# Turning every list's rows with TensorE's transposes, in a graph layer with a mixture of experts

## The chip, the core and the metric

The kernel runs on one core of a Trainium2 chip, in one launch. The metric is device time in microseconds (us), the median of several executions. Five engines work side by side, each through its own instructions in order: TensorE (PE, with its weight loads shown as PEld), VectorE (DVE), ScalarE (ACT), GpSimd (POOL) and SyncE (SP). DMA transfers are issued from SP's and POOL's streams.

## What is computed

3,327 tokens of 256 features pass a graph attention layer and then a mixture of 16 experts, of which each token uses two. Cut to what matters (`_layernorm` without scale and shift; everything in float32):

```python
# graph layer, on h = _layernorm(x) @ W, 4 heads of 64
attn = softmax(where(adj > 0, e, -9e15))       # e depends on the row and the head alone
x = x + layernorm(attn @ h) * gamma + beta
# experts, on x_n = _layernorm(x)
probs = softmax(x_n @ gate_w + gate_b)
top_probs, top_idx = top_k(probs, 2)           # two experts a token
hidden = silu(x_n @ w1[e]) * (x_n @ w2[e])     # 256 -> 512, for each expert e
x = x + sum over the token's two experts of  weight * (hidden @ w3[e])
```

## The kernel before

**The graph layer.** Tokens lie in 26 tiles of 128, in 7 groups. The adjacency matrix is streamed in and multiplied with `h` split in two parts (lines 598 and 599); after each group its rows are finished, normalized, gated and stored to a DRAM tensor `normed`, and their numbers are put into lists by expert.

**The lists.** The experts' work is cut into 19 lists of token numbers, 0 to 18, with room for `ROOM[i]` tokens (line 89). Lists 0 to 2 hold the tokens of three experts from the first five groups, lists 3 to 5 those of the same experts from the last two, and lists 6 to 18 (480, 472, 416 and so on down to 336 tokens from list 8 on) the other 13 experts, the fullest first. `take_list` (line 1143) writes the work of one list:

- *Gather* (line 970): one indirect DMA on POOL for each tile of 128 rows, from `normed` into one of three buffers (`XE[i % 3]`). A weighing on DVE (lines 976 and 978) takes the tokens' weights from the gathered rows.
- *Turning*: the products need the rows with features on partitions. Lists 0 to 7 use TensorE's transposes (line 1174) into a bank of PSUM, two of 128 x 128 for each tile of rows, and ACT copies each half (k = 0, 1) to the tile `xt` (line 1183). Lists 8 to 18 go through `by_halves` (line 1116): ACT and DVE split the 32-bit words into 16-bit halves (lines 1137 and 1138), SP issues a DMA transpose for each tile (line 1128), and ACT and DVE join the halves in `xt` (lines 1140 and 1141). `TURNED = 2 * EARLY + 2 = 8` is the first list that does so.
- *Up products*: lists 0 to 5 plainly (line 985). Lists 6 to 18 use seven products in the place of eight for each pair of column blocks (`by_sevenths`, line 996), two pairs a list, after a scheme that needs four sums of the weights and four of `xt` on DVE (line 1018). In a pair, p1, p5, p6, p2, p7, p3, p4 form a chain through copies on ACT (line 1052) and sums on DVE (line 1056): p6 needs p1's copy, p7 a sum of p6 and p5, p4 a copy of p7. p1, p6 and p7 write a bank of the pool `pt`, of two banks, which the transposes use as well.
- *Gate*: ACT's silu (line 1078) and DVE's product (line 1081) make `hid`.
- *Down products* (line 1099; a last tile of 64 rows or fewer packs its matmuls side by side, line 1095): for each tile of 128 rows into one of two `ph` banks. ACT scales full tiles by the tokens' weights to `y` (line 1222), DVE the small ones (lines 1224 and 1226); there are six `y` buffers.
- *Scatter* (line 1102): one indirect DMA on POOL for each tile adds `y` to the output's rows. A list's scatters follow the landing of the list before, since two lists may hold the same token.

A list's weights (1.5 MB) are loaded from SP's stream into one of four buffers.

**What sets the order.** Every step is added to a plan (class `Plan`, line 116) with an engine, a cost, a rank, what it follows and which buffers it takes. The planner places at each turn the step that can start first by these costs; rank decides between steps that can start together (lower goes first). It tries 80 orders, keeps the one that ends first in replays, and the instructions are then written in that order, each engine following its own. A cost thus changes no instruction, only its place. The rank of list i's down products is `(4, i + 1, 9, t)` from list 6 on (line 1212), that of its up products `(4, i, pair, number)`: the down products of list i fill gaps of the chain of list i + 1 and come behind it.

Of the kernel before, what the change touches and what calls it, by code (L numbers as in the profile page):

```python
# [77 lines left out]
CT = CAP // P  # L78
EARLY = 3
EARLY_GROUP = 4  # L80
TURNED = 2 * EARLY + 2

SEVEN = 2 * EARLY

NL = NE + EARLY
LIST = 4096
NR = NE - EARLY

# [130 lines left out]
def gnn_moe(ctx: ExitStack, tc: tile.TileContext, x, adj_t, W, a, gamma, beta, gate_w, gate_b, w1, w2, w3, out):  # L219
    nc = tc.nc  # L220
# [54 lines left out]
    column = const.tile([P, P], F32, name="column")  # L275
    piece = const.tile([P, NL, CT], F32, name="piece")
    code = const.tile([P, NT], F32, name="code")
    listed = const.tile([P, NL, CT], F32, name="listed")
    nc.vector.memset(listed, 0.0)
# [3 lines left out]

    count = const.tile([P, NL], F32, name="count")
    expert = const.tile([P, NL], F32, name="expert")
    behind = const.tile([P, NL], F32, name="behind")
    end = const.tile([P, NL], F32, name="end")
    room = const.tile([P, NL], F32, name="room")
# [6 lines left out]
    def constants():  # L295
# [10 lines left out]

        ramp(base, [[0, 2], [LIST // P, NE]], 0, 0)
        ramp(base[:, 1, :EARLY], [[LIST // P, EARLY]], NE * LIST // P, 0)

        ramp(column, [[1, P]], 0, 0)  # L310
        ramp(piece, [[LIST // P, NL], [1, CT]], 0, 0)
        ramp(expert[:, :2 * EARLY], [[0, 2], [1, EARLY]], 0, 0)
        for k in range(2):
            ramp(behind[:, k * EARLY:(k + 1) * EARLY], [[LIST, EARLY]], k * NE * LIST, 0)
        for i, n in enumerate(ROOM):
# [34 lines left out]
    PE, DVE, ACT, POOL, SP = "PE", "DVE", "ACT", "POOL", "SP"  # L350
# [61 lines left out]
    plan = Plan(SLOTS, take)  # L412
# [470 lines left out]
    def all_lists(counted, lists):  # L883
# [46 lines left out]
        def rest():  # L930
# [5 lines left out]
            nc.vector.tensor_reduce(count[:, 2 * EARLY:], by, AX.X, ALU.add)  # L936
            nc.vector.tensor_scalar(behind[:, 2 * EARLY:], expert[:, 2 * EARLY:], float(LIST), None, op0=ALU.mult)
            nc.vector.tensor_scalar(end, behind, float(LIST), None, op0=ALU.add)
            nc.vector.tensor_add(behind, behind, room)
# [56 lines left out]
    def by_sevenths(i, n, xts, loaded, fixed, xtk, wk, hk, weights):  # L996

        half = n // 2
        xsk, wsk, ask = ("xsum", i), ("hp", "list", i), ("agg", "list", i)
# [20 lines left out]
        def sums(cost, rank, after, uses, terms):  # L1020
            done, got = {}, []
            for k, (name, dst, one, other, op, needs) in enumerate(terms):
                done[name] = plan.add(DVE, cost, rank, after + [done[x] for x in needs],
                                      lambda dst=dst, one=one, other=other, op=op: combine(dst, one, other, op), uses)
            return done

        S = sums(0.62, (2, i, 7), loaded, [wk, wsk, ask], [
            ("1", lambda: ws(0), lambda: a(1, 0), lambda: a(1, 1), ALU.add, ""),
            ("2", lambda: ws(1), lambda: ws(0), lambda: a(0, 0), ALU.subtract, "1"),
            ("3", lambda: a(1, 0), lambda: a(0, 0), lambda: a(1, 0), ALU.subtract, "1"),  # L1030
            ("4", lambda: ws(2), lambda: a(0, 1), lambda: ws(1), ALU.subtract, "2")])
        X_ = sums(0.1 + 0.55e-3 * n, (2, i, 6), xts, [xtk, xsk, ask], [
            ("1", lambda: xs(0), lambda: b(0, 1), lambda: b(0, 0), ALU.subtract, ""),
            ("2", lambda: xs(1), lambda: b(1, 1), lambda: xs(0), ALU.subtract, "1"),
            ("3", lambda: b(0, 1), lambda: b(1, 1), lambda: b(0, 1), ALU.subtract, "1"),
# [2 lines left out]
        hids = []  # L1038
# [77 lines left out]
    def by_halves(i, got, tiles, xek, xtk, opened):  # L1116

        hk, tk = ("halves", i), ("turned", i)
        nt, m = len(tiles), len(tiles) * P

        def words(h):
            return XE[i % 3][:, :nt, :D].bitcast(U16).rearrange("p t (d h) -> p t d h", h=2)[:, :, :, h]

        def halves_of(h):
            return T[hk][:, :nt, h, :]

        def turn(t):
            nc.sync.dma_start_transpose(out=T[tk][:, :, t * P:(t + 1) * P], in_=T[hk][:, t].rearrange("p h d -> p (h d)"))

        def joined(h):  # L1130
            return T[xtk].rearrange("p (a b) k q -> p a (b k q)", a=KC).bitcast(U16).rearrange(
                "p a (n h) -> p a n h", h=2)[:, :, :m, h]

        def turned(h):
            return T[tk][:, h * KC:(h + 1) * KC, :m]

        s = [plan.add(ACT, 0.1 + 0.23 * nt, (1, i), got + opened[:1], lambda: nc.scalar.copy(halves_of(0), words(0)), [xek, hk]),
             plan.add(DVE, 0.1 + 0.15 * nt, (2, i, 8), got + opened[:1], lambda: nc.vector.tensor_copy(halves_of(1), words(1)), [xek, hk])]  # L1138
        w = [plan.add(SP, 1.3, (1, i), s, lambda t=t: turn(t), [hk, tk], landing=2.7, size=2 * P * D * 4) for t, _ in tiles]
        return [plan.add(ACT, 0.1 + 1.25e-3 * m, (1, i), w, lambda: nc.scalar.copy(joined(0), turned(0)), [tk, xtk], slack=2.0),  # L1140
                plan.add(DVE, 0.1 + 1.3e-3 * m, (2, i, 8), w, lambda: nc.vector.tensor_copy(joined(1), turned(1)), [tk, xtk], slack=2.0)]

    def take_list(i, indexed, stored, weights, opened, order):

        n = ROOM[i]
        tiles = row_tiles(n)
        xek, xtk, hk, wk = ("xe", i), ("xt", "list", i), ("hid", i), ("w", weights)
        limit = NP if i >= EARLY else (GROUPS[EARLY_GROUP][-1] + 1) * P
        rank = (4, i)
# [8 lines left out]
        def w_of(k):  # L1158
            return WE[weights][k]

        got = GOT[i] = [plan.add(POOL, 1.33, (1, i), [indexed] + stored, lambda t=t: gather(XE[i % 3], index_of(i), t, limit), [xek],
                        landing=2.6) for t, _ in tiles]
# [9 lines left out]
        def turned(k):  # L1172
            for t, _ in tiles:
                nc.tensor.transpose(psum(("pt", "list", i, k))[:, t * P:(t + 1) * P], XE[i % 3][:, t, k * P:(k + 1) * P], ident)

        m = len(tiles) * P
        xts = []
        if i >= TURNED:
            xts = by_halves(i, got, tiles, xek, xtk, opened)
        for k in range(KC if i < TURNED else 0):  # L1180
            key = ("pt", "list", i, k)
            w = plan.add(PE, 0.13 * len(tiles), rank + (0,), got, lambda k=k: turned(k), [key, xek])
            xts.append(plan.add(ACT, 0.1 + 0.9e-3 * m, (1, i), [w], lambda k=k, key=key: nc.scalar.copy(
                xt()[:, k, :m], psum(key)[:, :m]), [key, xtk]))
        hids = []
        if i >= SEVEN:
            if i == SEVEN:
                CHAIN.append(plan.add(PE, 0.9, (4, i, -1), UPS, fix_banks, [("pa", "fixed", r) for r in range(4)]))
            hids = by_sevenths(i, n, xts, opened, CHAIN[0], xtk, wk, hk, weights)
        for j in range(JC if i < SEVEN else 0):  # L1190
# [12 lines left out]
            s = plan.add(ACT, 0.1 + 0.95e-3 * n, (1, i), [ups[0]], gate, [keys[0], ("gate", i, j)])  # L1203
            hids.append(plan.add(DVE, 0.1 + 1.1e-3 * n, (2, i), [s, ups[1]], both, [keys[1], ("gate", i, j), hk]))
        ends = []
        for t, mm in tiles:
            key, yk = ("ph", "list", i, t), ("y", i, t)
            parts = (0, 1) if i >= SEVEN and PARTS[mm] == 1 else (None,)
            w = None
            for part in parts:  # L1210
                w = plan.add(PE, (8 * 0.217 / PARTS[mm] + 0.1 * (PARTS[mm] > 1)) / len(parts),
                             (4, i + 1, 9, t) if i >= SEVEN else rank + (9 + t,), hids + [w],
                             lambda t=t, mm=mm, key=key, part=part: down_products(psum(key), w_of(2), hid(), t, mm, part),
                             [key, hk] + ([wk] if weights else []))


            helped = (i < EARLY or i >= SEVEN) and PARTS[mm] == 1

            def scale(t=t, mm=mm, key=key, yk=yk, helped=helped):
                weight = T["weight", i][:mm, t:t + 1]  # L1220
                if helped:
                    nc.scalar.mul(T[yk][:mm], psum(key)[:mm, :D], weight)  # L1222
                else:
                    nc.vector.tensor_scalar(T[yk][:mm], psum(key)[:mm, :D], weight, None, op0=ALU.mult)
                for c in range(P // PARTS[mm], P, P // PARTS[mm]):
                    nc.vector.scalar_tensor_tensor(T[yk][:mm], psum(key)[c:c + mm, :D], weight, T[yk][:mm],
                                                   op0=ALU.mult, op1=ALU.add)

            w = plan.add(ACT if helped else DVE, 0.48 * PARTS[mm], (2, i), [w, wd], scale, [key, yk, ("weight", i)])
            ends.append(plan.add(POOL, 1.87, (1, i), [w] + order, lambda t=t, mm=mm, yk=yk: add_rows(  # L1230
                T[yk], index_of(i, out_index), t, mm, others, i < EARLY), [yk], landing=2.5))
# [13 lines left out]
    for t in range(GT):  # L1245
        LOADED[0, t] = plan.add(SP, 0.45, (0, t), [], lambda t=t: load_x(0, t, t + 1), landing=2.0, size=P * D * 4)
        if t == 0:
            got = plan.add(SP, 0.45, (0, t), [], lambda: nc.sync.dma_start(
                a_rows, bass.AP(tensor=a.tensor, offset=a.offset, ap=[[DH, 2], [1, DH]])), landing=2.0, size=512)
# [7 lines left out]
    for made, c0, c1, c in ((landed, H, H + D, 1.0), (summed, 0, H, 0.5)):  # L1257
        means, subtract = center(w_sb, ("ph", "w", c0), c0, c1)
        w = plan.add(PE, c, (0,), [made], means, [("ph", "w", c0)])
# [11 lines left out]
    w = plan.add(PE, 0.8, (2,), [rest], means, [("ph", "gw")])  # L1271
# [7 lines left out]
    for g in range(NG):  # L1279
# [3 lines left out]
        s, c, l, d = finish(g, terms, add_beta(g, read[g]), tables)  # L1283
# [3 lines left out]
        if g == EARLY_GROUP:  # L1287
            i, c = early_lists(c, l)
            tables = [c]
            ready.update({k: (i, list(stored)) for k in range(EARLY)})  # L1290
        if g == NG - 1:
            i, ranked, o = all_lists(c, l)
# [22 lines left out]
    opened = plan.add(PE, 0.0, (9,), every, switch_pools)  # L1315
# [23 lines left out]
    with tc.If(many["value"] > 0):  # L1339
        with tc.For_i(0, NL) as i:  # L1340
            e = nc.values_load(table[0:1, 0, bass.ds(i, 1)], min_val=0, max_val=NE - 1)
            full = nc.values_load(table[0:1, 1, bass.ds(i, 1)], min_val=0, max_val=1)
            w = weight_tiles()
            load_weights(w, e)
            with tc.For_i(0, full * (NT // AGAIN)) as c:
# [11 lines left out]
                n = AGAIN * P  # L1357
# [6 lines left out]
                for j in range(JC):  # L1364
# [3 lines left out]
                    s = POOLS["gates"].tile([P, CAP], F32, name="s")  # L1368
# [42 lines left out]
```

## Time and profile before

| | |
|---|---|
| median of three executions | 529.54 us (526.9 to 530.24) |
| the profiled execution | 529.58 us, of which 527.4 from its first to its last instruction (the span) |
| mean granted TensorE clock | 0.982 of full speed |
| the lists' gathers, line 970 | 61, 1,078 ns mean on POOL, 4.7 us median to landing |
| the scatters, line 1102 | 61, 1,661 ns mean on POOL, 4.3 us median to landing |
| DMA transposes, line 1128 | 41, 3.6 us median to landing |
| TensorE's transposes, line 1174 | 40, 277 ns mean |
| copies from PSUM to `xt`, line 1183, 128 x 512 | 4, 588 ns mean |
| splitting, 128 x 1024 halves | ACT 1,044 ns, DVE 714 ns mean |
| joining, 128 x 1024 halves | ACT 1,335 ns, DVE 773 ns mean |

The profile is one execution on the chip. Its page gives the busy time of each engine, the span in 40 equal slices (a digit is the busy share of a slice in tenths; PEclk is the granted clock), and groups of equal instructions. The trace gives windows (the same for any stretch) and the timeline: start, duration, engine, line, operation, destination and sources, and in brackets how long the engine stood before the row and what ended that. Matmuls follow each other closer than their durations say, because they are pipelined; a float32 product is shown as two matmuls, a transpose as one. Releasers are inferred, and a few matmul records are missing.

### The profile page before, as it was taken

Reading aid. Unit: us, or ns where it says so; the run is one execution under the profiler, and the core shown is the slowest. Engines: PE = TensorE matmul, PEld = TensorE weight load, DVE = VectorE, ACT = ScalarE, POOL = GpSimd, SP = SyncE. Lnnn points to the kernel's source line nnn. Section 1 sums busy time; section 2 is a strip of 40 time slices with the busy share of each in tenths; the row PEclk is TensorE's granted clock in tenths of the full one; section 3 lists DMA queues with packets and bytes.
Section 4 is the critical chain, followed back from the end, with each engine's and each line's share of the span. In section 5 each row is a group of like instructions: output and inputs, shape, how many; then the busy total and the mean of one; then the engine's idle time right before and its main releaser. Section 6 shows DMA issues by size and latency. Waiting matters only on the chain. (4 is left out here: it accounts for less than half of the span.)

```text
span 527.4 us, 9541 instructions
## 1 busy us (share of the span) xinstructions
PE 497.3 (94%) x3239; PEld 449.5 (85%) x3240; DVE 349.0 (66%) x1035; ACT 235.2 (45%) x637; POOL 222.1 (42%) x240
## 2 busy tenths in 40 slices
PE   9999999999999999999999799898799989999991
PEld 6789999999999999777778589797688879989990
DVE  5978563977869799679844496646548656877320
ACT  2452154536371760573222466545435454454440
POOL 4220022211031412756786578365375544444333
PEclk9999999999999999999999899999989998999996
DMA  8933879797869895563399659594595877642222
GB/s 273 356 131 101 291 268 293 255 332 240 276 209 367 263 370 157 196 183 99 64 293 322 95 134 118 159 211 78 167 215 83 210 238 170 131 122 30 24 30 34
DMA packets 85703, 100.06 MB, mean 190 GB/s; under 512 B 27150, under 2 KB 59154, under 8 KB 85652
## 3 DMA queue, kind: packets, MB, share of 16 engines
q1 hardware_dynamic: 74612, 85.42, 51.9%
q0 software_dynamic: 10768, 13.75, 16.2%
q8 instruction: 26, 0.43, 0.3%
q10 hardware_dynamic: 272, 0.26, 0.1%
q14 instruction: 25, 0.20, 0.1%
HBM read 81.55 MB, written 13.75 MB: 181 GB/s over the span
## 5 line engine op out<-in xcount | busy, mean ns | idle before, releaser
L598 PE MATMUL pa<-hi,mk 128*128 128x258 f32 x676 | 167.6, 289 | 0.0
L599 PE MATMUL pa<-lo,mk 128*128 128x256 f32 x676 | 163.2, 282 | 0.0
L1102 POOL DMA_INDIRECT out<-y,out_index x61 | 101.3, 1661 | 106.2 <-ACT y L1222 68.8
L598 PEld LDWEIGHTS pa<-hi,mk 128*128 128x128 f32 x676 | 127.9, 189 | 1.1 <-issue 1.0
L599 PEld LDWEIGHTS pa<-lo,mk 128*128 128x128 f32 x676 | 127.7, 189 | 0.1
L1099 PE MATMUL ph<-w3e,hid 128*128 128x256 f32 (+5 forms) x400 | 97.2, 386 | 7.1 <-ACT y L1222 7.0
L1099 PEld LDWEIGHTS ph<-w3e,hid 128*128 128x128 f32 (+5 forms) x400 | 74.3, 190 | 18.6 <-ACT y L1222 9.0
L970 POOL DMA_INDIRECT x<-normed,index x61 | 65.8, 1078 | 27.7 <-issue 18.0
L575 DVE TENSOR_SCALAR mk<-sg 128x2048 fp32r<-128x2048 f32 (+2 forms) x49 | 54.2, 1106 | 28.9 <-PE pa L599 28.2
L1046 PE MATMUL pt<-xt,w12e 128*128 128x256 f32 (+8 forms) x208 | 47.4, 353 | 2.2 <-DVE pa L1056 2.2
L1078 ACT ACTIVATE s<-pa 128x256 f32<-128x256 f32 (+8 forms) x78 | 26.8, 345 | 43.6 <-PE pa L1046 41.4
L1046 PEld LDWEIGHTS pt<-xt,w12e 128*128 128x128 f32 x208 | 37.4, 194 | 7.0 <-DVE pa L1056 2.9
L664 POOL TENSOR_TENSOR hp<-csum,c 128x512 f32<-128x512 f32 (+1 forms) x14 | 15.1, 1096 | 65.0 <-DVE c L660 65.0
L1081 DVE TENSOR_TENSOR hid<-s,pa 128x256 f32<-128x256 f32 (+8 forms) x78 | 28.8, 371 | 14.7 <-ACT s L1078 13.6
L1222 ACT ACTIVATE y<-ph,weight 128x256 f32<-128x256 f32 (+4 forms) x50 | 23.1, 470 | 33.0 <-PE ph L1099 31.7
L1052 ACT COPY pa<-pt 128x512 f32<-128x512 f32 (+8 forms) x52 | 25.1, 498 | 17.8 <-PE pt L1046 15.3
L1056 DVE TENSOR_TENSOR c<-pt,qs 128x512 f32<-128x512 f32 (+8 forms) x26 | 15.5, 596 | 25.5 <-ACT pa L1052 25.5
L492 PE MATMUL ph<-w_sb,xnt 128*128 128x260 f32 x104 | 27.9, 405 | 0.6 <-DVE lo L498 0.6
L985 PE MATMUL pa<-xt,w12e 128*128 128x352 f32 (+3 forms) x128 | 26.8, 360 | 0.0
L1046 PE MATMUL pa<-xsum,w12e 128*128 128x256 f32 (+8 forms) x104 | 22.9, 343 | 1.6 <-ACT pa L1052 1.6
L1138 DVE COPY halves<-x 128x1024 uint16<-128x1024 uint16 (+1 forms) x11 | 7.8, 708 | 25.1 <-DMA x<-normed,index 24.8
L1056 DVE TENSOR_TENSOR pa<-pt,qs 128x512 f32<-128x512 f32 (+8 forms) x26 | 15.7, 602 | 12.7 <-PE pt L1046 12.1
(213 smaller groups left out, 842.5 us busy)
## 6 DMA issues: line engine op xcount, KB each, us to landing
sg<-in_adj_t SPq DMA_DIRECT2D x25, 1024.0 KB, 6.2
sg<-in_adj_t SPq DMA_DIRECT2D x20, 768.0 KB, 5.4
w12e<-in_ffn_w SPq DMA_DIRECT2D x30, 512.0 KB, 5.0
w3e<-in_ffn_w SPq DMA_DIRECT2D x15, 512.0 KB, 7.0
normed<-pay SPq DMA_DIRECT2D x5, 520.0 KB, 7.4
out<-x SPq DMA_DIRECT2D x5, 512.0 KB, 5.8
sg<-in_adj_t SPq DMA_DIRECT2D x4, 576.0 KB, 4.8
x<-in_x SPq DMA_DIRECT2D x4, 512.0 KB, 8.6
```

What stands on the lines that cost most here:

```text
L492: nc.tensor.matmul(ph[:, :H + D], T["xnt", g, t][:, k, :], w_sb[:, k, :], start=(k == 0), stop=(k == KC - 1))
L575: nc.vector.tensor_scalar(T[mk][:, :m, :n * P], T[sk][:, :m, :n * P], 0.0, None, op0=ALU.is_gt)
L598: nc.tensor.matmul(pa[:, :D + 2], lhs, HI[mg][:, i, H:], start=first, stop=False)
L599: nc.tensor.matmul(pa[:, :D], lhs, LO[mg][:, i, H:], start=False, stop=left[g, t] == 0)
L970: nc.gpsimd.indirect_dma_start(out=xe[:, t, :], out_offset=None, in_=normed[:limit], in_offset=at_rows(idx, t), bounds_check=limit - 1, oo ...
L985: nc.tensor.matmul(p[:, :n], wt[:, k, j * P:(j + 1) * P], xt[:, k, :n], start=(k == 0), stop=(k == KC - 1))
L1046: nc.tensor.matmul(psum(key)[:, w * (CAP // 2):w * (CAP // 2) + half], lhs()[:, w, jp], rhs(), start=first and w == 0, stop=True, skip_gro ...
L1056: return plan.add(DVE, 0.16 + 1.02e-3 * n, (1, i, jp), after, lambda: nc.vector.tensor_tensor(dst(), both(psum(xx)), T[qs][:, :, :half], o ...
L1078: nc.scalar.activation(T[gk][:, t * half:(t + 1) * half], part(0), AF.Silu)
L1081: nc.vector.tensor_mul(T[hk][:, 2 * jp + j, t * half:(t + 1) * half], T[gk][:, t * half:(t + 1) * half], part(1))
L1099: nc.tensor.matmul(py[:m, :D], hid[:, j, t * P:t * P + m], w3e[:, j, :], start=(j == 0), stop=(j == JC - 1))
L1102: i = nc.gpsimd.indirect_dma_start(out=out, out_offset=at_rows(idx, t, m), in_=y[:m], in_offset=None, bounds_check=NP - 1, oob_is_err=Fals ...
```

## The change

`TURNED` becomes `NL` = 19, so no list goes through `by_halves`; lists 8 to 18 are turned like lists 0 to 7. The down products of the last two lists (17 and 18) get the rank `(4, i, 9 + t)`, which puts those of list 17 ahead of list 18's chain. The planner's costs of DVE's sums are set anew (0.62 to 0.69, and 0.1 + 0.55e-3 n to 0.16 + 0.5e-3 n, in us), as are costs inside `by_halves`, which is not called any more.

```diff
-TURNED = 2 * EARLY + 2
-
 SEVEN = 2 * EARLY
 
 NL = NE + EARLY
+TURNED = NL
...
-        S = sums(0.62, (2, i, 7), loaded, [wk, wsk, ask], [
+        S = sums(0.69, (2, i, 7), loaded, [wk, wsk, ask], [
...
-        X_ = sums(0.1 + 0.55e-3 * n, (2, i, 6), xts, [xtk, xsk, ask], [
+        X_ = sums(0.16 + 0.5e-3 * n, (2, i, 6), xts, [xtk, xsk, ask], [
...
-        s = [plan.add(ACT, 0.1 + 0.23 * nt, (1, i), got + opened[:1], lambda: nc.scalar.copy(halves_of(0), words(0)), [xek, hk]),
-             plan.add(DVE, 0.1 + 0.15 * nt, (2, i, 8), got + opened[:1], lambda: nc.vector.tensor_copy(halves_of(1), words(1)), [xek, hk])]
+        s = [plan.add(ACT, 0.1 + 0.23 * nt, (1, i), got + opened[:1], lambda: nc.scalar.copy(halves_of(0), words(0)), [xek, hk], slack=4.0),
+             plan.add(DVE, 0.1 + 0.16 * nt, (2, i, 8), got + opened[:1], lambda: nc.vector.tensor_copy(halves_of(1), words(1)), [xek, hk], slack=4.0)]
...
-        return [plan.add(ACT, 0.1 + 1.25e-3 * m, (1, i), w, lambda: nc.scalar.copy(joined(0), turned(0)), [tk, xtk], slack=2.0),
-                plan.add(DVE, 0.1 + 1.3e-3 * m, (2, i, 8), w, lambda: nc.vector.tensor_copy(joined(1), turned(1)), [tk, xtk], slack=2.0)]
+        return [plan.add(ACT, 0.1 + 2.4e-3 * m, (1, i), w, lambda: nc.scalar.copy(joined(0), turned(0)), [tk, xtk], slack=3.0),
+                plan.add(DVE, 0.1 + 1.35e-3 * m, (2, i, 8), w, lambda: nc.vector.tensor_copy(joined(1), turned(1)), [tk, xtk], slack=3.0)]
...
-                             (4, i + 1, 9, t) if i >= SEVEN else rank + (9 + t,), hids + [w],
+                             (4, i + 1, 9, t) if SEVEN <= i < NL - 2 else rank + (9 + t,), hids + [w],
```

In the order in which the new kernel is built, PE's instructions are the same as before up to list 7's transposes. From there on the transposes of list i + 1 stand between the chains of list i and list i + 1, followed by the down products of list i's first tile (of all its tiles for list 17). On POOL the gathers of lists 11 to 18 stand among the scatters of lists 6 to 13 (before, the last gather, list 18's, stood ahead of list 12's scatters). On DVE the weighing of a list's rows stands two to three lists ahead of that list's chain.

## The prediction

> **What bounds the kernel now.** I read the page's first two parts, then the table of windows by stage, then the timeline of the last 240 us with every engine, and last the timeline of the end.
>
> ```profile
> PE 497.3 (94%) x3239; PEld 449.5 (85%) x3240; DVE 349.0 (66%) x1035; ACT 235.2 (45%) x637; POOL 222.1 (42%) x240
> PE   9999999999999999999999799898799989999991
> PEclk9999999999999999999999899999989998999996
> ```
>
> TensorE is the bound: about full up to slice 21 (285 us), and then dented. The dents lie in the lists' stage. Windows (columns: length, busy us and count of PE, PEld, DVE, ACT, POOL, then granted clock, DMA share, GB/s):
>
> ```profile
> 292.00:298.00 6.00, 4.75 (x14) 3.88 (x15) 2.76 (x8) 3.18 (x7) 4.73 (x4) 0.72 0.75 100
> 376.00:387.00 11.00, 7.61 (x29) 5.79 (x28) 5.76 (x13) 4.39 (x9) 4.67 (x3) 0.84 0.48 93
> 430.00:441.00 11.00, 9.24 (x46) 8.12 (x45) 6.82 (x15) 4.28 (x9) 6.20 (x4) 0.84 0.51 118
> 440.00:515.80 75.80, 75.80 (x435) 69.25 (x434) 43.38 (x109) 35.84 (x88) 30.77 (x20) 1.00 0.43 81
> ```
>
> From 440 us on, when no more rows are split, PE never stands. Before that it does, and the clock falls too. One dent in the timeline, list 10's end (start, length, then engine, line, operation; brackets: idle time before it and what ended it):
>
> ```profile
> 377.25 0.85 PE L1046 MATMUL pt<-xt,w12e 128*128 128x204 f32 x4
> 378.35 1.04 ACT L1137 COPY halves<-x 128x1024 uint16<-128x1024 uint16 x1 [3.84 <-DMA x<-normed,index]
> 378.40 0.69 DVE L1138 COPY halves<-x 128x1024 uint16<-128x1024 uint16 x1 [3.49 <-DMA x<-normed,index]
> 380.98 0.83 ACT L1222 ACTIVATE y<-ph,weight 128x256 f32<-128x256 f32 x2
> ...
> 381.50 5.41 PE L1099 MATMUL ph<-w3e,hid 128*128 128x256 f32 x16 [3.39 <-ACT y L1222]
> ```
>
> The splitting copies stand on ACT and DVE behind a gather that has not landed. Gates, products into `hid` and the scaling of `y` are queued behind them, so both `ph` banks stay taken and PE stands 3.39 us; then the halved clock stretches the next 16 matmuls from 3.8 to 5.41 us. The end (POOL's rows are the last scatters):
>
> ```profile
> 507.88 7.93 PE L1099 MATMUL ph<-w3e,hid 128*128 128x256 f32 x36
> ...
> 511.55 1.62 POOL L1102 DMA_INDIRECT out<-y,out_index  x1 [0.30 <-issue]
> ...
> 518.92 1.57 POOL L1102 DMA_INDIRECT out<-y,out_index  x1 [5.75 <-issue]
> 520.79 1.57 POOL L1102 DMA_INDIRECT out<-y,out_index  x1 [0.30 <-issue]
> 522.67 1.44 POOL L1102 DMA_INDIRECT out<-y,out_index  x1 [0.30 <-issue]
> ```
>
> PE is done at 515.8. List 18's three scatters wait until list 17's have landed (513.17 to 518.92, 5.75 us), because PE does list 17's down products only after list 18's chain.
>
> **The sum is made in the profiled execution**: span 527.4, time 529.58, so 2.2 us lie around the span; the median of three, 529.54, is the same. In the order in which the two kernels are built, every PE instruction up to list 7's first half of transposes is the same, so all before 285 us stays.
>
> **1. Stops that go.** For each row of the PE timeline from 285 us on I took the time to the next row less its matmuls at the spacing of undisturbed ones (0.216 us for 256 columns, in proportion below). What is left over stands in nine places: at 290.3 (2.09), 301.1 (1.81), 336.4 (1.58), 356.2 (2.39), 377.3 (3.56), 413.2 (1.17), 421.9 (0.45) and 431.1 (1.92): 14.97 us, with under 0.2 each elsewhere, which I leave alone. The granted clock costs 6 x 0.28 + 11 x 0.16 + 11 x 0.16 = 5.2 us more in the three windows; each fall follows a stop of 1.8 us or more.
>
> The first two stops mostly stay. At 291.5 DVE waits for list 8's gather not only with the copy but also with the weighing of its rows (line 976, a wait of its own of 5.9 us in 10 rows), which in the new order stands ahead of list 6's sum that p7 needs; at 301.7 the same with list 9. Without the copies (0.69 on DVE) the chain of list 7 starts about 0.6 us sooner, with list 8's first four transposes done in the shadow. So of 14.97 + 5.2 I take off 0.6 here and, from the other six places, 11.07 + 3.52: **15.2 us**.
>
> **2. Transposes added.** Lists 8 to 18 have 41 tiles of rows, so 82 transposes; four are in the shadow above. Eight in a row took 1.04 us with 0.273 for the last one (line 1174), so 0.110 apart: 78 x 0.110 = **+8.6 us**, all on PE's path. Ends: nothing, if they fell into idle time, which step 1 has used up; and 78 x 0.273 = 21.3 if none overlapped. I take 0.110, since the built order has them in runs of four, six and eight like the row.
>
> **3. The new wait behind them.** Each list's chain now waits for transposes, then ACT's two copies (0.59 each, line 1183), then DVE's four sums of `xt`. In the built order the eight matmuls' worth of list i-1's first down tile (1.73 us) stand between the transposes and the chain. From the last transposes' end: copies done after 0.6 to 1.2 us, against 1.73. The second product needs the first sum 0.7 us later still; DVE reaches that sum behind a small tile's scaling (0.47 + 1.51 us, lines 1224 and 1226), which by my count ends 0.8 us before it is needed. So nothing; the other end, with that cover gone, is 1.2 + 0.4 us for each of ten lists, 16 us. The copies also lie on ACT ahead of that tile's `y`, whose `ph` bank was free 2 us before.
>
> **4. Splitting, DMA transposes, joining removed.** ACT loses 1.04 + 1.34 us a list and gains 1.17, DVE loses 0.71 + 0.77, SP loses 41 transposes in whose line weight loads stood. Neither engine was the bound (45% and 66%): nothing beyond step 1. ACT's and DVE's costs in the code's plan change no duration.
>
> **5. The last two lists.** List 17's down products (24 matmuls, 5.2 us) move ahead of list 18's chain. They no longer fill that chain: its last product ends, and the down products wait for gate and multiply; before, p4 started at 507.31 and the last `hid` was ready at 508.81, so PE stands 508.9 - 507.9 = 1.07, and about 0.1 before p4 (p7 to its copy's end took 1.24, with 1.14 of products between): **+1.2 us**. In exchange list 17's scatters are issued some 9 us earlier. Counted from the end of list 17's chain (T): list 16's last scatter is issued at T + 1.7, ends at 3.3, lands at 9.0; list 17's three then take 9.0 to 14.3 (1.87 apart), land at 20.0; list 18's first `y` is there at 18.2, so its scatters start at 20.0, the last at 23.8. PE ends at T + 20.9. So 2.9 us from PE's end to the last scatter's start, against 522.67 - 515.8 = 6.9: **-4.0 us**. At the ends: 0, if list 16's scatters are as late as list 17's were, and -5.6, if y alone decides.
>
> Sum: 527.4 - 15.2 + 8.6 + 1.2 - 4.0 = 518.0; with 2.2 around it **520 us**.
>
> One rule speaks against this. The row first: the twelve transposes at 283.9 to 286.0 ran with the clock at 1.00 in the window 286 to 292, and it fell only after the 1.93 us stop. The Trainium skill (TensorE: Matmul & The Clock Gate, Part 4: PE-mode transpose) says that transposes do not count as busy time for the clock gate as matmuls do. By that rule each list's group could bring a half-clock stretch; by the row none comes, since a group is 0.9 us between full matmul work. It stands as rival D.
>
> **The rivals.**
> A. *The gathers become the wait (slower).* Before, a list's gather buffer was free once its halves were copied, up to five lists ahead. Now a gather waits for PE's transposes three lists back, and in POOL's built order gather 11 to 15 stand among the scatters of lists 6 to 11; one tile even behind a scatter that waits for the landing of the list before (5.75 us). The weighing of that list stands in DVE ahead of the next chain's sums. My count for gather 12: last tile issued at 353, landed after 4.7 us (the median) by 358; weighing reached at 360, needed by 364. So it decides once POOL runs 6 us late; scatters landed up to 8.4 us after issue, gathers up to 6.8, which is near. Then stops as long as now stay: 520 + 14.6 = 535.
> B. *The tail does not shorten*: list 17's scatters wait on list 16's so long that the last again follow 6.9 us behind PE: 524. Against it, 16's last `y` comes 20 us before PE's end.
> C. *The cover of step 3 is short* by 0.5 to 0.6 us a list: 526. For it, DVE's margin there is under 1 us; against it, the products are 0.64 to 0.7 us apart and the first needs no sum.
> D. *The clock falls with each group of transposes*: a half-clock stretch is 3.41 us in this trace, so 1.7 us lost, times 11: 539.
> E. *The first two stops go as well*, since without DMA transposes on the queues the gathers of lists 8 and 9 land some us sooner: 3.9 us and a half-clock stretch at most, so 516.
>
> **How the numbers follow.** Forecast 0.60, A 0.08, B 0.08, C 0.10, D 0.04, E 0.10. About 1% (524.2 to 534.8) is what a measurement of this kernel can tell from no change. Faster by over 1%: forecast, E and three quarters of B, 0.76; within: C and the rest of B, 0.12; slower: A and D, 0.12. The predicted time is the likeliest case's, 520. The range runs from E, 516, less a little for a tail gain of 5.6, to C with 1 us more: 515 to 527; that leaves A and D out.
>
> **What would show it.** Rows of the transposes: 122 in all, 0.27 us each, eight within 1.1 us. The dents in slices 25 to 33 gone, PE without a stop over 0.5 us from 305 to 495, the clock 1.00 there; list 18's chain starting near 495 instead of 497.3; PE's end near 510; about 3 us from there to the last scatter. It would be wrong if PE's waits name the gather, the weighing or the copies at the lists' borders by more than 6 us in all, if PE is done after 514, or if list 18's first scatter still has over 4 us of idle time while its `y` is ready.

## The result, and the profile after

The kernel after takes 514.84 us (median of 4 runs, 514.65 to 515.5), the kernel before beside it 528.89 (4 runs, 526.9 to 530.24): a ratio of 0.974, with a 95% interval of 0.9705 to 0.9774. The profiled execution has a span of 513.8 us against 527.4. The page of the kernel after, its first two parts:

```profile
PE 499.5 (97%) x3321; PEld 453.9 (88%) x3322; DVE 336.0 (65%) x1013; ACT 227.4 (44%) x637; POOL 220.2 (43%) x240
PE   8899999999999999999998999999999999999995
PEclk9999999999999999999999999999999999999998
```

PE has 82 instructions more than before. The dents in slices 25 to 33 are gone, and so is every fall of the clock but the one behind PE's last matmul. The same shows in the windows of the kernel after (columns as in the windows of before; the last ends with PE's work):

```profile
292.00:298.00 6.00, 5.04 (x24) 4.12 (x23) 3.38 (x8) 3.03 (x7) 3.85 (x4) 1.00 0.34 64
376.00:387.00 11.00, 11.00 (x65) 10.51 (x64) 4.27 (x12) 5.66 (x13) 7.02 (x6) 1.00 0.77 212
430.00:441.00 11.00, 11.00 (x64) 10.54 (x62) 5.91 (x16) 5.36 (x14) 6.33 (x5) 1.00 0.59 150
440.00:507.50 67.50, 67.50 (x401) 61.13 (x399) 37.56 (x94) 31.96 (x80) 30.26 (x21) 1.00 0.37 65
```

Only the first stretch still has a stop. Where list 11's chain begins, the timeline of the kernel after reads (start, length, then as before):

```profile
376.89 1.04 PE L1173 MATMUL pt<-ident,x 128*128 128x128 f32 x8
...
377.53 1.07 ACT L1182 COPY xt<-pt 128x512 f32<-128x512 f32 x2
377.77 1.89 PE L1098 MATMUL ph<-w3e,hid 128*128 128x256 f32 x8
...
379.20 0.36 DVE L1017 TENSOR_TENSOR xsum<-xt,agg 128x204 f32<-128x204 f32 x1
379.50 0.85 PE L1045 MATMUL pt<-xt,w12e 128*128 128x204 f32 x4
379.70 0.47 ACT L1221 ACTIVATE y<-ph,weight 128x256 f32<-128x256 f32 x1 [1.09 <-PE ph L1098]
```

(From `SEVEN` on a line's number is one less than before.) Eight transposes occupy PE from 376.89 to 377.77, ACT's two copies are done at 378.6, the four sums at 379.56, and the chain starts at 379.50 with no idle time: the eight matmuls between cover the copies, and the second product, at 380.19, comes 0.6 us after the last sum. The end of the kernel after:

```profile
489.08 1.61 POOL L1101 DMA_INDIRECT out<-y,out_index  x1 [2.12 <-ACT y L1221]
493.80 1.56 POOL L1101 DMA_INDIRECT out<-y,out_index  x1 [3.11 <-DMA out<-y,out_index]
...
502.16 5.34 PE L1098 MATMUL ph<-w3e,hid 128*128 128x256 f32 x24
...
502.77 0.33 DVE L1080 TENSOR_TENSOR hid<-s,pa 128x168 f32<-128x168 f32 x1
504.97 1.57 POOL L1101 DMA_INDIRECT out<-y,out_index  x1 [5.81 <-ACT y L1221]
...
508.70 1.43 POOL L1101 DMA_INDIRECT out<-y,out_index  x1 [0.30 <-issue]
```

POOL stands 3.11 us ahead of list 17's first scatter, until list 16's last one has landed, where before it stood 5.75 us ahead of list 18's for list 17's. List 18's scatters now wait for nothing but their own `y`. The last starts 508.70 - 507.50 = 1.2 us after PE's end; before it was 522.67 - 515.81 = 6.86.

So the 13.6 us of span come together: from list 6's first transposes to PE's end 231.7 us before and 221.6 after, -10.1; the tail -5.7; that stage started 1.8 us later in the profiled run after (285.90 against 284.11), though both kernels have the same instructions up to there; and from the last scatter's start to the span's end it took 0.4 longer.

### The profile page after: what moved, and what is told of

Read it like the earlier page. It is cut to its first block, busy times and chain, and to the rows that moved or that the text cites. A ratio compares the mean times of both kernels' runs of the same rounds, so it can differ in the third digit from the quotient of the medians.

```text
span 513.8 us, 9646 instructions
## 1 busy us (share of the span) xinstructions
PE 499.5 (97%) x3321; PEld 453.9 (88%) x3322; DVE 336.0 (65%) x1013; ACT 227.4 (44%) x637; POOL 220.2 (43%) x240
## 5 line engine op out<-in xcount | busy, mean ns | idle before, releaser
L1101 POOL DMA_INDIRECT out<-y,out_index x61 | 97.6, 1600 | 96.0 <-ACT y L1221 57.9
L1098 PE MATMUL ph<-w3e,hid 128*128 128x256 f32 (+5 forms) x400 | 95.4, 379 | 0.0
L1098 PEld LDWEIGHTS ph<-w3e,hid 128*128 128x128 f32 (+5 forms) x400 | 72.9, 187 | 8.9
L969 POOL DMA_INDIRECT x<-normed,index x61 | 67.3, 1103 | 25.5 <-issue 15.2
L1045 PE MATMUL pt<-xt,w12e 128*128 128x256 f32 (+8 forms) x208 | 45.7, 342 | 1.0 <-DVE pa L1055 1.0
L984 PEld LDWEIGHTS pa<-xt,w12e 128*128 128x128 f32 x128 | 19.3, 191 | 5.7 <-issue 1.2
```

Of the source, the lines that this page charges most:

```text
L969: nc.gpsimd.indirect_dma_start(out=xe[:, t, :], out_offset=None, in_=normed[:limit], in_offset=at_rows(idx, t), bounds_check=limit - 1, oo ...
L984: nc.tensor.matmul(p[:, :n], wt[:, k, j * P:(j + 1) * P], xt[:, k, :n], start=(k == 0), stop=(k == KC - 1))
L1045: nc.tensor.matmul(psum(key)[:, w * (CAP // 2):w * (CAP // 2) + half], lhs()[:, w, jp], rhs(), start=first and w == 0, stop=True, skip_gro ...
L1098: nc.tensor.matmul(py[:m, :D], hid[:, j, t * P:t * P + m], w3e[:, j, :], start=(j == 0), stop=(j == JC - 1))
L1101: i = nc.gpsimd.indirect_dma_start(out=out, out_offset=at_rows(idx, t, m), in_=y[:m], in_offset=None, bounds_check=NP - 1, oob_is_err=Fals ...
```

## The experiments

Two theories stood after the result. **Theory of place**: TensorE's stops came from the splitting copies, which the plan had written into ACT's and DVE's orders ahead of gathers that had not landed; the change helps because it takes these copies away. **Rival**: the new costs, which the prediction set at nothing, or the traffic of the DMA transposes, did it. The first four kernels ran beside one measurement of the kernel before (530.82 us, 12 runs).

**The new rank alone, in the kernel before.**

```diff
-                             (4, i + 1, 9, t) if i >= SEVEN else rank + (9 + t,), hids + [w],
+                             (4, i + 1, 9, t) if SEVEN <= i < NL - 2 else rank + (9 + t,), hids + [w],
```

> The kernel before with one line changed: the last two lists' down products get the rank ahead of the last chain; lists 8 to 18 are still split and turned by DMA transposes. Theory (the gain is two separate things, PE's stops and the tail): PE ends 0.3 us later, as in the changed kernel's chain of list 18, and the last scatter starts 1.4 us behind it instead of 6.9, so 5.2 us faster than before, about 523.7. Rival (the tail shortens only because the stage ahead of it has no splitting): no change, 528 to 530.

Measured: 526.48 us (8 runs), ratio 0.990 (0.986 to 0.994). The time lies between the two expectations; against the kernel before beside it, it is 4.3 us less by the medians, which is nearer to the theory's 5.2 than to no change. PE's end to the last scatter is 1.2 us here too.

**All but the new rank** (the kernel after with the old one).

> The changed kernel with the old rank of the down products: all lists turned by TensorE, list 17's down products again in and behind list 18's chain. Theory: the tail's 5.2 us come back, about 520, with PE ending near 507 as in the changed kernel. Rival: the down products in list 18's chain hide something there, and the time stays at 515.

Measured: 518.42 us (4 runs), ratio 0.9793 (0.9759 to 0.9826), nearer to the theory than to the rival. From PE's end (505.92) to the last scatter (511.27) it takes 5.35 us, against 1.2 in the kernel after: the rank is worth about 4 us there as well.

**Halves and DMA transposes back, with the new costs, slacks and rank.**

```diff
-TURNED = NL
+TURNED = 2 * EARLY + 2
```

> The changed kernel with TURNED back at 8: lists 8 to 18 split and joined again, but with the changed kernel's costs and slacks in the plan and with the rank of the last two lists. Theory (the copies stand in ACT's and DVE's order behind gathers, whatever the plan believes): stops remain and the time is that of the run with the rank alone, 520 to 525. Rival (the new costs and slacks, by putting instructions in other places, are what removed the stops): about 515 to 517, with no stop of PE over 1 us after 305.

Measured: 513.25 us (4 runs), ratio 0.9683 (0.9644 to 0.9722). This was the surprise: with not one transpose added, and all the copies and DMA transposes still there, it is no slower than the kernel after (the intervals overlap), and faster than the rival's 515 to 517, although PE still stands once for 3.94 us, from 316 us on. So what the title of the change names was not needed for the gain. Either the costs or the slacks had done what the rank, worth some 4 us, had not.

**Each transpose of lists 8 to 18 issued twice**, in the kernel after.

```diff
-                nc.tensor.transpose(psum(("pt", "list", i, k))[:, t * P:(t + 1) * P], XE[i % 3][:, t, k * P:(k + 1) * P], ident)
+                for _ in range(2 if i >= 8 else 1):
+                    nc.tensor.transpose(psum(("pt", "list", i, k))[:, t * P:(t + 1) * P], XE[i % 3][:, t, k * P:(k + 1) * P], ident)
```

> The changed kernel with every transpose of lists 8 to 18 issued twice into the same bank, 82 more. Theory (PE is the bound throughout and a transpose costs its spacing): 82 x 0.110 = 9.0 us more, about 524. Rival (the transposes lie in time that PE would lose anyway): 515 to 517. If transposes drew the clock down: a granted clock under 0.98 and more than 9 us.

Measured: 525.45 us (5 runs), ratio 0.9905 (0.9866 to 0.9944). Against the kernel after, 82 more transposes cost 10.6 us by the medians and 8.7 by the two ratios, so 0.11 to 0.13 us each: they are not free. All other instructions stand in the kernel after's order, by the traces' rows. Group and window of this kernel:

```profile
L1174 PE MATMUL pt<-ident,x 128*128 128x128 f32 x168 | 20.8, 274 | 0.0
310.00:440.00 130.00, 130.00 (x730) 119.90 (x729) 70.84 (x166) 60.23 (x138) 73.97 (x54) 1.00 0.52 131
```

In groups of sixteen they still leave the clock at 1.00 and PE without idle time in this window.

The next four kernels ran beside another measurement of before (531.22 us, 13 runs). First **the slack of the splitting copies alone**, in the kernel before; everything else, costs, rank, joining, as it was:

```diff
-... lambda: nc.scalar.copy(halves_of(0), words(0)), [xek, hk]),
-... lambda: nc.vector.tensor_copy(halves_of(1), words(1)), [xek, hk])]
+... lambda: nc.scalar.copy(halves_of(0), words(0)), [xek, hk], slack=4.0),
+... lambda: nc.vector.tensor_copy(halves_of(1), words(1)), [xek, hk], slack=4.0)]
```

> The kernel before, with one thing changed: the plan may not place a splitting copy until 4.0 us after its gathers are planned to have landed (a slack of 4.0 on both copies). Halves, DMA transposes and joining stay, as do all costs and the old rank of the last two lists. Theory (the stops come from splitting copies written into ACT's and DVE's order ahead of gathers that have not landed; where the copies stand later, nothing queues behind them): their waits for the gathers, 15.0 us on ACT and 18.1 on DVE before, fall below 4 us each, TensorE's stops after 305 us (11.1 us) and the half-clock stretches (3.5 us) mostly go; the tail stays long, so the run with all new costs and slacks, 513.2, plus the 4 us of the tail: 517 us (514 to 520). Rival (the new costs of the sums and of the joining move the chains' sums, and the slack alone does little): 526 to 530.

Measured: 510.75 us (4 runs), ratio 0.9668 (0.9584 to 0.9752), less than the 514 to 520 expected. No instruction is added, removed or changed. The copies stand later in two engines' orders, and since the whole order is planned anew, others move with them: some 75 of PE's 3,239 instructions, 70 of DVE's 1,035 and 15 of ACT's 638 stand elsewhere among the rest. The groups of the copies between 310 and 440 us, first in the kernel before (after the bar: busy us, mean ns, then idle time just before them and what ended it):

```profile
L1137 ACT COPY halves<-x 128x1024 uint16<-128x1024 uint16 (+1 forms) x9 | 8.8, 972 | 15.0 <-DMA x<-normed,index 15.0
L1138 DVE COPY halves<-x 128x1024 uint16<-128x1024 uint16 (+1 forms) x9 | 6.4, 711 | 18.4 <-DMA x<-normed,index 18.1 <-issue 0.2
```

and with the slack:

```profile
L1137 ACT COPY halves<-x 128x1024 uint16<-128x1024 uint16 (+1 forms) x9 | 8.7, 968 | 0.0
L1138 DVE COPY halves<-x 128x1024 uint16<-128x1024 uint16 (+1 forms) x9 | 6.2, 686 | 0.6 <-issue 0.2
```

The copies take as long as before and wait for nothing. PE's window, before and with the slack:

```profile
310.00:440.00 130.00, 119.85 (x605) 107.50 (x604) 80.35 (x180) 65.91 (x138) 73.70 (x54) 0.98 0.73 160
```

```profile
310.00:440.00 130.00, 130.00 (x695) 119.31 (x694) 91.16 (x210) 74.19 (x154) 79.22 (x57) 1.00 0.87 182
```

PE is full at a clock of 1.00 while the DMA engines are busier than before (0.87 against 0.73): more traffic did not stop it. From list 6's first transposes to PE's end it takes 213.7 us, 18.0 less than before and 7.9 less than the kernel after, which pays 9.0 for 82 transposes. The tail is the long one, 6.8 us.

**The costs alone**, in the kernel before (the sums' 0.69 and 0.16 + 0.5e-3 n, and the three inside `by_halves`; no slack, old rank).

> The kernel before, with the plan's new costs alone: the sums (0.69 and 0.16 + 0.5e-3 n), the splitting on DVE (0.16 a tile) and the joining (2.4e-3 and 1.35e-3 a token); the slacks and the rank stay as before. Theory (the copies' place ahead of the landing is the cause, and a cost moves it only by accident): the copies still wait for gathers by over 8 us on each engine, 524 to 530 us. Rival (the costs did it): 515 to 519.

Measured: 525.34 us (10 runs), ratio 0.9924 (0.9882 to 0.9965), in the theory's range. ACT's and DVE's copies wait 12.4 and 13.4 us for gathers from 305 us on, as the theory has it. But the costs move more than it allows: the order is another from 85 us on, in the graph layer, and in the profiled run list 6's transposes start 5.9 us later than before, from where PE needs 219.9 us, 11.8 less. Its stops after 305 us add up to 5.8 us, against 10.1 before by the same rows. So the time that the copies wait does not by itself tell how long PE stands.

**The old costs of the sums in the kernel after.**

> The kernel after, with the plan's old costs of DVE's sums (0.62 and 0.1 + 0.55e-3 n): TensorE transposes and the new rank stay. Theory (without splitting copies nothing in the order waits for a gather ahead of the chain, so the sums' costs matter little): as the kernel after, 514.8 (513.5 to 517). Rival (the sums' costs are what keeps the sums in time): 519 to 525, with TensorE's stops named after the sums on DVE.

Measured: 514.45 us (4 runs), ratio 0.9724 (0.9647 to 0.9801): the same as the kernel after. By the traces every engine's instructions stand in the kernel after's order, so this run is a repeat of that kernel: the new costs of the sums decide nothing there.

**The weighing later**, in the kernel after.

```diff
-        wd = plan.add(DVE, 0.4, (2, i, 9), got, weighed, [xek, ("weight", i)])
+        wd = plan.add(DVE, 0.4, (2, i, 9), got, weighed, [xek, ("weight", i)], slack=4.0 if i >= SEVEN else 0.0)
```

> The kernel after, with a slack of 4.0 us on the weighing of the rows of lists 6 to 18, so that it is written later in DVE's order. Theory (TensorE's first stop at 293 us, 0.96 us idle after, 1.93 before, is the weighing of list 8 waiting for its gather ahead of a sum that p7 needs): that stop and the one at 302 (0.47) go, 513.5 us (512.5 to 515). Rival (a weighing that stands later frees the gather buffers later, so that the gathers after it come late): 516 to 519.

Measured: 511.39 us (4 runs, 511.09 to 511.88), ratio 0.9659 (0.9586 to 0.9732), below the theory's range; the kernel after and its repeat took 513.29 to 516.14 in eight runs. The two stops that the kernel after still has, as its timeline shows them:

```profile
292.97 0.23 DVE L975 SCALAR_TENSOR_TENSOR hit<-x,expert 128x8 f32<-128x8 f32 x1 [4.20 <-DMA x<-normed,index]
...
294.07 1.13 PE L1045 MATMUL pt<-xt,w12e 128*128 128x256 f32 x4 [0.96 <-DVE pa L1055]
...
300.75 0.23 DVE L975 SCALAR_TENSOR_TENSOR hit<-x,expert 128x8 f32<-128x8 f32 x1 [2.03 <-DMA x<-normed,index]
...
302.15 0.66 PE L1173 MATMUL pt<-ident,x 128*128 128x128 f32 x4 [0.47 <-DVE c L1055]
```

are gone: a weighing that stood ahead of its gather's landing held PE as the copies had, through the sum behind it. PE needs 219.2 us from list 6's transposes on (221.6 after).

The last three ran beside a third measurement of before (529.61 us, 13 runs). **The copies put back without their purpose**: the kernel after plus the splitting copies of lists 8 to 18 at the costs of before and without slack. What they write is used by nothing; there is no DMA transpose and no joining.

```diff
+        if i >= 8:
+            hv, nt = ("halves", i), len(tiles)
+            for eng, h, cost, rk in ((ACT, 0, 0.1 + 0.23 * nt, (1, i)), (DVE, 1, 0.1 + 0.15 * nt, (2, i, 8))):
+                plan.add(eng, cost, rk, got + opened[:1], lambda h=h, eng=eng: (nc.scalar.copy if eng == ACT else nc.vector.tensor_copy)(
...
```

> The kernel after, with the splitting copies of lists 8 to 18 put back on ACT and DVE at the costs and without the slack of before; what they write is used by nothing, there are no DMA transposes and no joining, and TensorE turns the rows. Theory (the place of these copies in the two engines' orders, ahead of the gathers' landing, is what stops TensorE, whatever turns the rows): the copies wait for gathers again, some 15 us on each engine, and most of the stops taken away (11.1 us and 3.5 of clock) come back: 524 to 530 us. Rival (the stops came from the whole of halves, DMA transposes and joining, by the traffic on the queues): within 3 us of the kernel after, 515 to 518.

Measured: 521.41 us (10 runs), ratio 0.986 (0.9819 to 0.9901): 6.6 us of the gain are lost again by the medians, and the time lies between the theory's range and the rival's. Three of the ten runs took 525.1 to 525.8 us, the other seven 519.6 to 521.8. The profiled run (525.07 us) is one of the three: PE's way from list 6's transposes on is 232.8 us there, 11 longer than in the kernel after. From 305 us on its copies wait 11.1 and 12.4 us for gathers, and PE's stops add up to 5.3 us, half of what they were before. This run comes nearest to moving the copies alone: beside them, four instructions of PE, four of DVE and six of ACT stand elsewhere than in the kernel after, and none of SP or POOL. The stop at list 10's end in this kernel:

```profile
378.21 1.89 PE L1098 MATMUL ph<-w3e,hid 128*128 128x256 f32 x8
379.99 1.04 ACT L1180 COPY halves<-x 128x1024 uint16<-128x1024 uint16 x1 [3.35 <-DMA x<-normed,index]
380.01 0.69 DVE L1180 COPY halves<-x 128x1024 uint16<-128x1024 uint16 x1 [4.68 <-DMA x<-normed,index]
...
382.03 3.06 PE L1098 MATMUL ph<-w3e,hid 128*88 128x256 f32 x8 [1.92 <-ACT y L1226]
```

It is the picture of before, at the same place, with nothing on the queues but gathers, scatters and weights. So the place of two copies of 1.0 and 0.7 us stops PE without any DMA transpose or joining, and the run with the slack, which keeps both, shows PE's window full. That the copies' place accounts for all of the stops of before is not shown: half of them came back.

**A later landing in the plan**, in the kernel before. The plan counts a gather's landing from the end of its POOL instruction, to which it gives 1.33 us. Counted from the instruction's start, as the trace counts it, the change is from 3.9 to 6.3 us, and the 4.7 us measured lies between.

```diff
-                        landing=2.6) for t, _ in tiles]
+                        landing=5.0) for t, _ in tiles]
```

> The kernel before, with one number of the plan changed: a gather is planned to land 5.0 us after its issue, not 2.6 (measured: 4.7 in the median). No slack, no cost, no rank changed. Theory (the plan put the copies too early because it believed in a landing of 2.6): copies and weighing stand later, their waits for gathers fall below 5 us on each engine after 305 us, the first two stops shrink too; the tail stays long: 508 to 514 us. Rival (the plan's own replays absorb a later landing by issuing the gathers earlier or by another order, and the copies stand as close to the landing as before): 520 to 528.

Measured: 515.78 us (4 runs), ratio 0.9765 (0.9703 to 0.9826), slower than the theory's 508 to 514. From 305 us on the copies wait 2.7 us for gathers on ACT and not at all on DVE, and PE needs 213.1 us from list 6's transposes on, as with the slack. But those transposes start 4.9 us later than before (288.98). As with the costs alone, the order is another from 85 us on; what in it costs the time I did not follow up.

**All three, without TensorE's transposes**: the slack on the copies, the slack on the weighing, and the new rank, in the kernel before.

> The kernel before, with a slack of 4.0 us in the plan on the two splitting copies and on the weighing of lists 6 to 18, and the new rank of the last two lists; halves, DMA transposes and joining stay, all costs stay. Theory (the three gains add up, and no transposes of 9 us are paid): 510.75 of the slack alone, less 3 for the first two stops, less 3.6 to 4.4 for the tail: 504 us (502 to 507), below every kernel so far. Rival (buffers come free later with a later weighing, or the tail is no longer the end): 508 to 513.

Measured: 504.9 us (4 runs, 503.58 to 508.19), ratio 0.9539 (0.9481 to 0.9597), as the theory had it: faster than both kernels, by 10 us than the kernel after. Page lines of this kernel:

```profile
PE 492.1 (97%) x3239; PEld 446.7 (88%) x3240; DVE 349.6 (69%) x1035; ACT 237.4 (47%) x637; POOL 220.6 (44%) x240
PEclk9999999999999999999999899999999999999999
```

The same 3,239 instructions on PE as before, from list 6's transposes to PE's end in 212.8 us, 18.9 less, and a tail of 1.2.

## Why the prediction was right, and where it was not

The sum was 520.0 and the kernel took 514.84, 0.2 under the range's lower end of 515. The sign, the bound and the mechanism held, and none of the signs of being wrong appeared: PE's waits at the lists' borders come to 1.4 us, it is done at 507.5, and list 18's first scatter waits for its own `y`. The sum was further off than the total says. In the profiled runs the way from list 6's transposes to PE's end and the tail shrank by 15.8 us, where the sum has 9.4; that the stage started 1.8 us later and the last landing took 0.4 longer was chance, and hid a part. Two slips change little: the stops listed are eight, not nine, and 508.9 - 507.9 is 1.0, not 1.07. The terms:

1. *Stops that go, -15.2.* Measured: from list 7's p1 (304.30 before, 302.65 after) to PE's end 211.5 and 204.85, with 8.6 of transposes and 0.3 in list 18's chain added, so 15.6 us went where I had 14.6. At the first two stops I had 0.6, and 3.9 went (20.19 us from list 6's transposes to that p1 before, 16.75 after, with 0.44 of transposes in it). This is the first mis-sized term: I reckoned that the weighing would hold the sums as long as the copies had. It did hold them, by 4.20 and 2.03 us on DVE, but only 0.96 and 0.47 of that reached PE, and no half-clock stretch followed, where one had followed the 1.93 us of before. Nor had the weighing waited 5.9 us at these two lists before: those waits, of 3.33 and 2.61 us, were at lists 6 and 7. How much of the 3.9 us is chance stands below the list.
2. *Transposes, +8.6.* Right: eight in 0.88 us, and the doubling of all 82 cost 10.6 us by the medians and 8.7 by the ratios, against the 9.0 expected.
3. *The wait behind them, 0.* Right, with the margin of 0.6 us seen above; rival C did not come.
4. *Splitting and joining, nothing more; "ACT's and DVE's costs in the code's plan change no duration".* The sentence is true and misled me. A cost or a slack changes no duration, but it changes the place, and step 1 hung on the place. I had read from the stop at 377 us that the copies stood behind a gather that had not landed, and then took for granted that they had to be taken away. The slack of 4.0 that the diff also adds, on a function that the new kernel does not call, is worth at least as much alone (0.9668, 0.9584 to 0.9752) as the change (0.974, 0.9705 to 0.9774). It does not alter the forecast for this kernel, since the function is not called, but it is the reading of the dents that a learner should take away.
5. *The last two lists, +1.2 on PE and -4.0 at the end.* Both mis-sized. On PE it cost 0.3 (list 18's chain 8.23 us, against 7.94 at the spacing of undisturbed products): the down products started at 502.16 while the last `hid` was ready at 503.10. They start with the `hid` of the first pair, which is ready long before; I had made all of them wait for the last gate. The tail gave 5.7, its other end: list 16's last scatter started 4.7 us ahead of list 17's first, not 7.3, so that `y` alone decides at list 18.

How much of the 3.9 us at the first two stops is the change and how much chance is open. Three more kernels have the order of the kernel after up to there. The first stop of the one with the old rank, and of the one with the transposes issued twice:

```profile
292.95 1.13 PE L1045 MATMUL pt<-xt,w12e 128*128 128x256 f32 x4 [2.64 <-DVE pa L1055]
```

```profile
294.06 1.27 PE L1045 MATMUL pt<-xt,w12e 128*128 128x256 f32 x4 [2.49 <-DVE pa L1055]
```

With the old costs it is 1.44 us. Only the 2.49 us were followed by a half-clock stretch (from 294.9), not the 2.64, so the length of a stop alone does not decide that. From list 6's transposes to list 7's p1 these executions take 18.2, 19.8 and 17.3 us, so with the transposes counted 1.3 to 3.9 us went at the first two stops, more than my 0.6 in each.

The 3.9 is the size of rival E, to which I gave 0.10. Its ground, gathers that land sooner, shows at the second stop: what waits for list 9's last gather starts 5.1 us after that gather's start before (296.64 to 301.77, with list 8's DMA transposes issued from 292.6 on) and 3.0 us after (297.74 to 300.75). E came in part, since the later weighing took a further 2.4 us of PE's way.

Rival A (gathers as the wait) speaks in the waits of the weighing, and PE was not held by it past 303 us. Rival B fell, by 1.2 against 6.86 us of tail. Rival D fell: the window 376 to 387 has eight transposes and a clock of 1.00, and so has 310 to 440 with the groups doubled. The Trainium skill (TensorE: Matmul & The Clock Gate, Part 4: PE-mode transpose) says that a transpose does not count as PE busy in the way a matmul does; groups of 0.9 and of 1.76 us between full matmul work show no sign of it here, and longer ones were not run.

How the copies came to stand ahead of the landing is shown in part. Gathers landed 2.3 us after the start of their POOL instruction at best, 4.7 in the median and 6.8 at worst in the kernel before, where the plan has 3.9. That difference does not make the whole wait. The last gather ahead of the copy at 378.35 us in the kernel before reads:

```profile
372.71 1.00 POOL L970 DMA_INDIRECT x<-normed,index  x1 [0.30 <-issue]
```

By the plan's figures it would have landed at 376.6. ACT stood from 374.5 on, so 2.1 of its 3.84 us would have been lost with that landing too: ACT had run ahead of POOL. The other 1.7 us are the later landing. A slack and a later landing in the plan both leave room for the two.

The Trainium skill (DMA: Bandwidth & Descriptors, Anatomy of one DMA) gives 2.0 us plus bytes over 436 thousand for a DMA of this path; for a tile of 128 rows of 1,040 bytes that is an estimate of 2.3 us. The fastest gather agrees, and the median does not. The DMA engines are 0.73 busy from 310 to 440 us; that this makes the difference is not shown.

## What to carry to other kernels

When an engine of strict order waits for a DMA, look at what stands behind that instruction, and ask whether moving it later is enough, before asking what could replace it. Check a planner's landings against the trace, counted from the same start, and leave room behind them: here two short copies without that room stood in the way of the bound engine. And an edit to a cost or a slack is to be predicted by the places it changes, one engine after the other, not by durations.

## What the runs showed that I had not expected

In the kernel with halves back and all re-planned, PE lost about 4 us at 316 us, and ACT's timeline reads:

```profile
313.39 1.04 ACT L1136 COPY halves<-x 128x1024 uint16<-128x1024 uint16 x1
319.84 0.57 ACT L1051 COPY pa<-pt 128x512 f32<-128x512 f32 x1 [5.41 <-remote]
```

The copy's source was written by p7, which PE had finished before 315, and the trace names no engine's instruction that released it. Gathers and a run of DMA transposes were being issued, and one packet of an instruction queue is recorded in that stretch (from 314.47, for 1.0 us). It may be that ACT waited for its own instructions; I did not try it, and it stays open. In the kernel with the copies' slack alone PE does not stop there.

List 6's first transposes started anywhere from 283.1 to 290.0 us in these profiles, up to 2.8 us apart (283.10 to 285.90) even among the six kernels with the same order up to there. So a comparison of two kernels' lists is better counted from that point than from the span's start.
